# Down weights quantised after an expert's silu products, thirteen gate and up tiles quantised in attention 2, four result buffers

## The chip, the cores and the metric

The kernel runs on one core of one Trainium2 chip. The metric is the device time of the whole program in microseconds (us), as the median over runs. One execution was also taken by the hardware profiler; its span runs from the first to the last instruction.

The engines are TensorE (PE: matmuls; PEld: its weight loads), VectorE (DVE), ScalarE (ACT), GpSimd (POOL) and SyncE (SP), which here only issues DMAs.

## The reference

Eight sequences of 100 tokens with 512 features (800 rows in all) pass through four blocks, each on a layer norm of `x` and each added to `x`:

```python
x = x + L0_xattn(layernorm(x), ctx)   # 16 heads of 32, causal, 100 keys
x = x + L0_ffn(layernorm(x))          # mixture of 8 experts, top 2, hidden size 352
x = x + L1_xattn(layernorm(x), ctx)   # "attention 2": 16 heads, latent keys, 361 keys, rope
x = x + L1_ffn(layernorm(x))          # quantised ffn, hidden size 1408
```

An expert computes `silu(x W1^T) * (x W2^T)` and multiplies that by `W3^T`; each token takes its two best experts, weighted by a softmax over the two scores.

The last block works on integers. Rows of `x`, of the hidden values and of both weight matrices are divided by a scale (their largest magnitude over 127), rounded, and the product is scaled back:

```python
scale = max(max(abs(v), axis=-1) / 127.0, 1e-8)
q = clip(round(v / scale), -127, 127)
```

Its weights are `w_gate_up` (2816 x 512: 22 tiles of 128 rows) and `w_down` (512 x 1408: 4 tiles of 128 rows).

## The kernel before

The program runs through its stages in order: attention 1 with the routing of tokens (up to about 143 us of the span), the experts (to about 283 us), the projections for attention 2, attention 2 over the eight sequences ("batches"; about 345 to 536 us), and the quantised ffn over seven row tiles, the output projection of attention 2 beside it (to the end).

*Weights of the last block.* They are quantised long before they are used, beside other stages. One gate and up tile (`gu`, 128 x 512) is loaded by SP, then VectorE takes the row maximum (`amax`, L147), makes scale and inverse (L135, L138), scales and rounds (L142) and writes bf16 integers (`gu_q`, L143); SP then turns it by a transposing DMA into `w1q` (L152). A down tile (`dn`, 128 x 1408) goes the same way through `dn_q` into `w2q`. `dn` and `dn_q` have one buffer each, so the next down tile is loaded only after the one before is quantised. The constant `LATER` says how many of the 22 gate and up tiles are left for attention 2; the others go through the experts, at most two for each expert (`quantise_next`), with three tiles in flight.

*One expert.* Up to 240 token rows, gathered into slots, were turned into columns (`xgT`) during the expert before. The hidden size is cut into three groups; `gate_and_up(m)` does the products of one (L1109), ScalarE applies silu (L1120, L1128), and VectorE multiplies into `hT` (L1121; for the third group L1129 to L1133). Then TensorE turns the rows of the next expert (L1040); their copies into `xgT` are shared, the first slot block by ScalarE (L1044), the second by VectorE (L1042). VectorE makes six small values for the next expert's gates and places (`choices`, L1025 to L1031). The down matmuls (L1175) read `hT`, and the results `y` (L1185 on ScalarE, L1183 on VectorE) are added to `x_acc` by scattering DMAs from POOL (L1186). Experts 0 to 3 also carry pieces of a weight fold for attention 2 (`fold_beside`, `fold_turn`, `fold_second`, `fold_third`).

In this stage the order of TensorE, VectorE and ScalarE is the order of the code (`manual_schedule`). SP is not in that list: its DMAs are put in order by the scheduler, and each waits in the queue behind the ones before it. An expert's weights are loaded two experts ahead into two buffers (L484, L487), the slot rows too (L1015).

*Attention 2.* Each batch has 13 tiles of scores: a matmul (L1379), the maximum (L1381), the exponential on ScalarE (L1385), the reciprocal and the scaling (L1387, L1388, on VectorE or POOL in turn), transposes (L1394), the values (L1406). At tiles 3 and 9 of a batch after the first, code for one of the left gate and up tiles is placed; here the scheduler may move instructions. The context of the next batch is turned at L1285, and batches 1, 3, 5 compute the next pair's queries (L1361).

*End of the last block.* Results of a row tile are scaled into `y` (L1668), the residual is added (L1671) and the tile is written out (L1672). `y` comes from a pool with two buffers. In the tail VectorE, ScalarE and TensorE again keep the order of the code.

Of the kernel before, what the change touches and what calls it, by code (L numbers as in the profile page):

```python
# [12 lines left out]
F32 = mybir.dt.float32  # L13
# [6 lines left out]
P = 128  # L20
B, S, D = 8, 100, 512
N = B * S
L, DC = 361, 128
KC = D // P
# [26 lines left out]
def tile_kernel(  # L51
# [9 lines left out]
    def open_pool(name, bufs=1, side="left"):  # L61
        guard = tc.tile_pool(name=name, bufs=bufs, side=side)
        pool = guard.__enter__()
        return pool, lambda: guard.__exit__(None, None, None)
# [6 lines left out]
    def bank(dtype=F32):  # L71
        cols = 512 if dtype == F32 else 1024
        return psum.tile([P, cols], dtype, tag="bank", name="bank")
# [653 lines left out]
    def fold_beside(i, wq_p, kq_p, qr_p):  # L727
        pa = bank()
        for c in range(CQ // P):
            for j in range(2):  # L730
                nc.tensor.matmul(
                    pa[ds(R1 * j, R1), :P], qr_p[:, j, c, :], kq_p[:, j, c, :],
                    start=(c == 0), stop=(c == CQ // P - 1),
                )
        t_p = fw.tile([P, P], F32, tag="t_p", name=f"t_p{i}", bufs=1)
        nc.scalar.copy(t_p, pa[:, :P])
        return i, wq_p, t_p
# [115 lines left out]
    def load_down(n):  # L853
        w = qin.tile([P, NI], F32, tag="dn", name=f"dn{n}", bufs=1)
        nc.sync.dma_start(w, wdn[ts(n, P), :])
        return n, w
# [21 lines left out]
    def turn_down(n, q):  # L878
        turn_by_dma(w2q[:, :, ts(n, P)], q)

    qin, close_qin = open_pool("weights_in")
    slot_rows, close_slot_rows = open_pool("slot_rows", bufs=2)
    LATER = 9
    gate_up_left = list(range(OT - LATER))
    HC = len(SLOTS)
    GB = 3
# [2 lines left out]
    def quantise_next():  # L889
        if gate_up_in:  # L890
            turn_gate_up(*quantise_gate_up(*gate_up_in.pop(0)))
            if gate_up_left:
                gate_up_in.append(load_gate_up(gate_up_left.pop(0)))
# [118 lines left out]
    def fetch(e, tiles=None):  # L1012
        got = []
        for i, xg in enumerate(tiles or slot_tiles(e)):
            d = nc.sync.dma_start(xg, x_slot[ds(1 + e * CAP + SLOTS[i][0], SLOTS[i][1]), :])  # L1015
            got.append((xg, d.ins))
        return got
# [63 lines left out]
    down_in = load_down(0)  # L1081
# [20 lines left out]
    for e in range(NE):  # L1102
        w12_e, w3_e = experts.pop(e)
        xgT = turned
        hT = ffw.tile([P, 3, CAP], F32, tag="hT", name=f"hT{e}")

        def products(po, cols, c0=0, c1=KC):
            for c in range(c0, c1):
                nc.tensor.matmul(  # L1109
                    po, w12_e[:, c, cols], xgT[:, c, :], start=(c == c0), stop=(c == c1 - 1)  # L1110
                )

        def gate_and_up(m):
            m0, mr = HCH[m]
            pw = bank()
            s = ffw.tile([P, CAP], F32, tag="silu", name="silu")
            if m < 2:
                products(pw[:, :CAP], ds(m0, P))
                products(pw[:, ds(CAP, CAP)], ds(UP[m], P))
                nc.scalar.activation(s, pw[:, :CAP], AF.Silu)  # L1120
                nc.vector.tensor_tensor(hT[:, m, :], s, pw[:, ds(CAP, CAP)], ALU.mult)  # L1121
                return
            products(pw[:, :CAP], ds(m0, P))
            for half in range(2):
                products(
                    pw[ds(64 * half, 64), ds(CAP, CAP)], ds(UP64, 64), 2 * half, 2 * half + 2
                )
            nc.scalar.activation(s[:mr], pw[:mr, :CAP], AF.Silu)  # L1128
            nc.vector.tensor_tensor(hT[64:mr, m, :], s[64:mr], pw[mr:, :CAP], ALU.mult)  # L1129
            up = ffw.tile([64, CAP], F32, tag="up", name="up", bufs=1)  # L1130
            nc.vector.tensor_copy(up, pw[:64, ds(CAP, CAP)])
            nc.vector.tensor_tensor(up, up, pw[64:, ds(CAP, CAP)], ALU.add)
            nc.vector.tensor_tensor(hT[:64, m, :], s[:64], up, ALU.mult)  # L1133

        slots.pop(e)
        if e + 2 < NE:
            slots[e + 2] = fetch(e + 2)
        part = None
        gate_and_up(0)
        if loaded:  # L1140
            part = fold_beside(*loaded.pop(0))
            if pairs_left:
                loaded.append(fold_load(pairs_left.pop(0)))
        quantise_next()
        gate_and_up(1)
        if part:
            part = fold_turn(*part)
        if e < KC:
            turn_down(*quantise_down(*down_in))
            if e + 1 < KC:  # L1150
                down_in = load_down(e + 1)
        gate_and_up(2)
        if part:
            part = fold_second(*part)
        quantise_next()
        if e + 2 < NE:
            experts[e + 2] = load_expert(e + 2)
        else:
            load_wo(*((0, 1, 2) if e + 2 == NE else (3, 4)))
        if e == KC + 1:  # L1160
            load_wo(5, 6, 7)
        if e + 1 < NE:
            turned = columns_of(e + 1, slots[e + 1])
            gates_next = choices(e + 1, slots[e + 1])
        if part:
            fold_third(*part)

        py = [bank() for _ in range(HC)]
        down = [(m, i) for m in range(len(HCH)) for i in range(HC)]
        if e == NE - 1:  # L1170
            down.sort(key=lambda a: a[1])
        for m, i in down:
            mr = HCH[m][1]
            s0, n = SLOTS[i]
            nc.tensor.matmul(  # L1175
                py[i][:n], hT[:mr, m, ds(s0, n)], w3_e[:mr, m, :], start=(m == 0), stop=(m == 2)
            )
        for i in range(HC):
            gate, place = gates[i]
            n = SLOTS[i][1]  # L1180
            y = rows.tile([P, D], F32, tag="xn", name=f"y{e}_{i}")[:n]
            if i % 2:
                nc.vector.tensor_scalar(y, py[i][:n], gate, None, ALU.mult)  # L1183
            else:
                nc.scalar.activation(y, py[i][:n], AF.Copy, scale=gate)  # L1185
            d = nc.gpsimd.indirect_dma_start(  # L1186
                out=x_acc, out_offset=bass.IndirectOffsetOnAxis(ap=place[:, 0:1], axis=0),
                in_=y, in_offset=None, compute_op=ALU.add,
            )
            tc.declare_no_dep(  # L1190
                d.ins, group=f"expert{e}", reason="a token has one slot at most of an expert"
            )
            tc.add_to_no_dep_group(f"expert{e}", d.ins)
        gates = gates_next
# [147 lines left out]
    a1w, close_a1w = open_pool("attn1w", bufs=2)  # L1342
    late_loads = [load_gate_up(OT - LATER + i, a1w) for i in range(2)]

# [89 lines left out]
    for b in range(B):  # L1434
# [7 lines left out]
        for i, (k0, r) in enumerate(BTILES):  # L1442
            e = scores(qe, kvT, k0, r, i % 2)
# [31 lines left out]
    f2w, close_f2w = open_pool("ffn1w", bufs=2)  # L1475
# [154 lines left out]
    def down4(t, hqT, sh):  # L1630
        pd = bank()
        for i, (g, c) in enumerate(CHUNKS4):
            for j in range(4):
                nc.tensor.matmul(
                    pd[ds(R4 * j, R4), :QD], hqT[:, c, ds(R4 * g, R4)], w2q[:, i, ts(j, QD)],
                    start=(i == 0), stop=(i == IT - 1),
                )
        y = f2w.tile([P, D], F32, tag="y", name="y")
        for j in range(4):
            nc.vector.scalar_tensor_tensor(  # L1640
                y[:R4, ts(j, QD)], pd[ds(R4 * j, R4), :QD], sh[:R4],
                swb[:R4, ds(OT * P + j * QD, QD)], ALU.mult, ALU.mult,
            )
        nc.vector.tensor_tensor(y[:R4], y[:R4], xs[t][:R4], ALU.add)
        nc.sync.dma_start(out[ds(t * P, R4), :], y[:R4])
# [17 lines left out]

    def finish_rows(t, pd, sh, y=None, cols=slice(0, D)):
        if y is None:
            y = f2w.tile([P, D], F32, tag="y", name="y")
        scale = swb[:, OT * P :]
        nc.vector.scalar_tensor_tensor(  # L1668
            y[:, cols], pd[:, cols], sh, scale[:, cols], ALU.mult, ALU.mult
        )  # L1670
        nc.vector.tensor_tensor(y[:, cols], y[:, cols], xs[t][:, cols], ALU.add)  # L1671
        nc.sync.dma_start(out[ts(t, P), cols], y[:, cols])  # L1672
# [60 lines left out]
    hqT = columns_of_hidden(t, q)  # L1733
    for u, _, s, pd in waiting[1:]:
        finish_rows(u, pd, s)
    y = f2w.tile([P, D], F32, tag="y", name="y")
    for cols in (slice(0, D // 2), slice(D // 2, D)):
        pd = bank()
        down_part(pd, hqT, 0, IT, cols)
# [71 lines left out]
```

## Time and profile before

| what | value |
|---|---|
| median of 3 runs | 674.64 us (672.87 to 675.77) |
| the profiled execution: its time | 681.28 us |
| the profiled execution: its span | 679.5 us |
| mean granted TensorE clock | 0.973 |
| ScalarE and POOL busy | 245.0 and 183.5 us |
| DMA traffic | 80.35 MB, mean 118 GB/s over the span |
| transposing DMA of a down tile, time on SP's queue (4 of them) | 4.1 to 8.2 us |
| transposing DMA of a gate and up tile (22 of them) | 1.2 to 3.4 us |

How to read it: the profiled execution is one run, and sums made from its durations belong to its own time. A group row of the profile names the line, the engine, the operation, the written and the read tile, how often it ran, its busy time and its idle time with what ended it. A row of the waits names who waited, on which line, for whom, then the total in us, how often, and the longest. A row of a timeline has the start and the length in us. A line number can be that of a helper, such as L147, which serves gate and up tiles as well as down tiles; the tile's name tells them apart.

### The profile page before, as it was taken

Reading aid. Unit: us, or ns where it says so; the run is one execution under the profiler, and the core shown is the slowest. Engines: PE = TensorE matmul, PEld = TensorE weight load, DVE = VectorE, ACT = ScalarE, POOL = GpSimd, SP = SyncE. Lnnn points to the kernel's source line nnn. Section 1 sums busy time; section 2 is a strip of 40 time slices with the busy share of each in tenths; the row PEclk is TensorE's granted clock in tenths of the full one; section 3 lists DMA queues with packets and bytes.
Section 4 is the critical chain, followed back from the end, with each engine's and each line's share of the span. In section 5 each row is a group of like instructions: output and inputs, shape, how many; then the busy total and the mean of one; then the engine's idle time right before and its main releaser. Section 6 shows DMA issues by size and latency. Waiting matters only on the chain.

```text
span 679.5 us, 9904 instructions
## 1 busy us (share of the span) xinstructions
PE 646.9 (95%) x3476; PEld 415.3 (61%) x3483; DVE 419.9 (62%) x1065; ACT 245.0 (36%) x565; POOL 183.5 (27%) x196
## 2 busy tenths in 40 slices
PE   8999997889998999999989999999999999999994
PEld 5766755666655677568866666666666544444442
DVE  4875697326655553353148877876677356666687
ACT  3654544322222111232145555555555313222140
POOL 2222231501110122138514243244234102221020
PEclk9999999589999999999989999999999999999998
DMA  9700393699999998654200211110000210011211
GB/s 292 249 18 17 119 322 108 241 309 220 299 295 302 253 326 214 140 175 120 84 1 15 59 44 21 53 36 12 0 13 0 90 38 20 18 30 29 49 37 63
DMA packets 80290, 80.35 MB, mean 118 GB/s; under 512 B 41267, under 2 KB 54119, under 8 KB 80111
## 3 DMA queue, kind: packets, MB, share of 16 engines
q1 hardware_dynamic: 76543, 70.97, 36.6%
q0 software_dynamic: 3696, 8.72, 6.0%
q8 instruction: 29, 0.48, 0.3%
q14 instruction: 22, 0.18, 0.1%
HBM read 56.36 MB, written 16.50 MB: 107 GB/s over the span
## 4 chain that ended last, share of the span: by engine, by line
PE 63%; DVE 7%; DMA 7%; POOL 1%; issue 1%; ACT 1%; SPq 0%; ACTq 0%; POOLq 0%; DVEq 0%
PE bank L359 12%; PE bank L1406 9%; PE bank L1379 9%; PE bank L1109 8%; PE bank L1325 6%; PE bank L1175 5%; PE bank L1394 5%; PE bank L1539 3%; DMA dn<-in_wdn 2%; PE bank L1361 1%; DMA gu<-in_wgu 1%; DMA qr_p<-in_wqr 1%; POOL e L1388 1%; DVE amax L147 1%; PE bank L711 1%
## 5 line engine op out<-in xcount | busy, mean ns | idle before, releaser
L1388 POOL TENSOR_SCALAR e<-e,rs 128x361 f32<-128x361 f32 (+1 forms) x56 | 67.2, 1201 | 131.9 <-DVE rs L1387 118.7
L359 PE MATMUL bank<-wvo,ctxT 128*128 128x512 f32 x192 | 83.9, 593 | 0.0
L1379 PE MATMUL bank<-kvT,qe 128*128 128x361 f32 (+1 forms) x208 | 83.0, 483 | 0.1
L1109 PE MATMUL bank<-xgT,w 128*128 128x240 f32 (+1 forms) x384 | 76.5, 373 | 1.6 <-ACT xgT L1044 0.9
L1109 PEld LDWEIGHTS bank<-xgT,w 128*128 128x128 f32 (+1 forms) x384 | 64.7, 183 | 14.4 <-issue 5.6
L1406 PE MATMUL bank<-pT,kvr 121*128 121x400 f32 x192 | 70.3, 502 | 1.0 <-DVE pT L80 1.0
L1394 PEld LDWEIGHTS bank<-ident,e 128*121 128x121 f32 (+1 forms) x312 | 48.3, 186 | 34.2 <-POOL e L1388 7.3
L1385 ACT ACTIVATE e<-bank,nm 128x361 f32<-128x361 f32 (+1 forms) x104 | 58.7, 565 | 27.2 <-DVE nm L1381 18.9
L1381 DVE TENSOR_REDUCE nm<-bank 128x1 f32<-128x361 f32 (+1 forms) x104 | 54.9, 528 | 15.8 <-PE bank L1379 14.6
L359 PEld LDWEIGHTS bank<-wvo,ctxT 128*128 128x128 f32 x192 | 36.2, 190 | 43.0 <-issue 42.6
L1186 POOL DMA_INDIRECT x_acc<-y,place x16 | 24.5, 1530 | 129.9 <-ACT y L1185 126.2
L1394 PE MATMUL bank<-ident,e 128*121 128x128 f32 (+1 forms) x312 | 53.0, 280 | 3.1 <-POOL e L1388 3.0
L1556 POOL TENSOR_TENSOR hid<-g,u 128x512 f32<-128x512 f32 (+1 forms) x17 | 20.5, 1216 | 111.0 <-ACT g L1547 74.8
L1175 PE MATMUL bank<-w,hT 128*128 128x512 f32 (+3 forms) x96 | 44.3, 607 | 4.0 <-DVE hT L1133 4.0
L1406 PEld LDWEIGHTS bank<-pT,kvr 121*128 121x128 f32 x192 | 33.9, 190 | 20.2 <-ACT pT L82 0.7
L1325 PE MATMUL bank<-xT,wqf 128*128 128x256 f32 (+1 forms) x192 | 43.8, 389 | 0.7 <-ACT xT L1310 0.7
L82 ACT COPY pT<-bank 121x384 f32<-121x384 f32 (+1 forms) x63 | 28.2, 447 | 42.4 <-PE bank L1394 42.3
L324 POOL TENSOR_TENSOR s<-s,rs 100x800 f32<-100x800 f32 x16 | 24.4, 1522 | 70.0 <-DVE rs L323 30.5
L1325 PEld LDWEIGHTS bank<-xT,wqf 128*128 128x128 f32 x192 | 36.3, 190 | 7.4 <-ACT xT L1310 0.9
L80 DVE COPY ctxT<-bank 128x400 f32<-128x400 f32 (+2 forms) x31 | 17.7, 572 | 37.0 <-PE bank L1325 26.0
L1379 PEld LDWEIGHTS bank<-kvT,qe 128*128 128x128 f32 (+1 forms) x208 | 32.9, 189 | 10.7 <-DVE rs L1387 0.5
L1175 PEld LDWEIGHTS bank<-w,hT 128*128 128x128 f32 (+3 forms) x96 | 16.8, 184 | 25.1 <-issue 16.6
(259 smaller groups left out, 1004.2 us busy)
## 6 DMA issues: line engine op xcount, KB each, us to landing
w<-in_w SPq DMA_DIRECT2D x8, 1408.0 KB
gu<-in_wgu SPq DMA_DIRECT2D x22, 256.0 KB
w<-in_w SPq DMA_DIRECT2D x16, 256.0 KB
wq_p<-in_wq SPq DMA_DIRECT2D x8, 512.0 KB
wo<-in_wo SPq DMA_DIRECT2D x8, 512.0 KB
x_slot<-zeros SPq DMA_DIRECT2D x1, 3840.0 KB
kq_p<-in_wkcq SPq DMA_DIRECT2D x16, 192.0 KB
dn<-in_wdn SPq DMA_DIRECT2D x4, 704.0 KB
```

Source lines behind the costliest of these rows:

```text
L82: nc.scalar.copy(dst, src)
L359: nc.tensor.matmul(po[:, :D], lhs[:, c, ds(t * P, r)], rhs[:, c, :], start=(c == 0), stop=(c == chunks - 1),)
L1109: nc.tensor.matmul(po, w12_e[:, c, cols], xgT[:, c, :], start=(c == c0), stop=(c == c1 - 1))
L1175: nc.tensor.matmul(py[i][:n], hT[:mr, m, ds(s0, n)], w3_e[:mr, m, :], start=(m == 0), stop=(m == 2))
L1186: d = nc.gpsimd.indirect_dma_start(out=x_acc, out_offset=bass.IndirectOffsetOnAxis(ap=place[:, 0:1], axis=0), in_=y, in_offset=None, compu ...
L1325: nc.tensor.matmul(pq[:, i, :], wqf[:, c, ts(p0 + i, P)], xT[:, c, :], start=(c == 0), stop=(c == KC - 1),)
L1379: nc.tensor.matmul(ps[:r, :L], qe[:, ds(k0, r)], kvT, start=True, stop=True)
L1381: d = nc.vector.tensor_reduce(nm[:r], ps[:r, :L], AX.X, ALU.max, negate=True)
L1385: nc.scalar.activation(e[:r], ps[:r, :L], AF.Exp, bias=nm[:r], accum_out=sm[:r])
L1388: (nc.vector if odd else nc.gpsimd).tensor_scalar_mul(e[:r], e[:r], rs[:r])
L1394: nc.tensor.transpose(pt[:LP, c, :r], e[:r, ds(c * (LP - 1), LP)], ident[:r, :r])
L1406: nc.tensor.matmul(pc[:, :VC], kvr[:, c, :], pT[:, c, :], start=(c == 0), stop=(c == LC - 1))
```

## The change

Three edits. In the experts, the quantisation of a down tile moves from between `gate_and_up(1)` and `gate_and_up(2)` to behind `gate_and_up(2)`, and from experts 0 to 3 to experts 1 to 4; the first down tile is still loaded before the experts begin, and the load of the next one follows the quantisation as before. `LATER` becomes 13, so nine gate and up tiles go through experts 0 to 4 (two in each of the first four, one in expert 4) and thirteen through attention 2. The result tile `y` of the last block gets four buffers. The order of instructions on TensorE, ScalarE and POOL is that of before; VectorE's and SP's change.

```diff
-    LATER = 9
+    LATER = 13
     gate_up_left = list(range(OT - LATER))
...
         gate_and_up(1)
         if part:
             part = fold_turn(*part)
-        if e < KC:
+        gate_and_up(2)
+        if 0 < e <= KC:
             turn_down(*quantise_down(*down_in))
-            if e + 1 < KC:
-                down_in = load_down(e + 1)
-        gate_and_up(2)
+            if e < KC:
+                down_in = load_down(e)
         if part:
             part = fold_second(*part)
         quantise_next()
...
-        y = f2w.tile([P, D], F32, tag="y", name="y")
+        y = f2w.tile([P, D], F32, tag="y", name="y", bufs=4)
...
-            y = f2w.tile([P, D], F32, tag="y", name="y")
+            y = f2w.tile([P, D], F32, tag="y", name="y", bufs=4)
...
-    y = f2w.tile([P, D], F32, tag="y", name="y")
+    y = f2w.tile([P, D], F32, tag="y", name="y", bufs=4)
```

## The prediction

> **What bounds the kernel now.** I read the page's busy row first, then the waits of TensorE and VectorE, then the chain of work that ended last, then the stretches that the change touches instruction by instruction. TensorE sets the pace: 646.9 of 679.5 us busy. What can be won is its 32.6 us of idleness and the time at a lower clock (mean granted clock 0.973, so about 0.027 x 679.5 = 18 us).
>
> ```profile
> PE 646.9 (95%) x3476; PEld 415.3 (61%) x3483; DVE 419.9 (62%) x1065; ACT 245.0 (36%) x565; POOL 183.5 (27%) x196
> ```
>
> Now the waits: TensorE's in the stretch 150 to 290 us (the experts), then VectorE's over the span (total, times, longest).
>
> ```profile
> PE bank L1175 <- DVE hT L1133: 4.0, 3, 2.9
> PE bank L1109 <- issue: 0.7, 1, 0.7
> ...
> DVE amax L147 <- DMA dn<-in_wdn: 7.4, 2, 4.7
> ...
> DVE y L1668 <- DMA out_y<-y: 0.7, 1, 0.7
> ```
>
> VectorE twice stood before the maximum of a down weight tile (`dn`) whose load had not landed; behind it in VectorE's queue stood the silu products `hT`, for which TensorE's down matmuls waited. The chain shows both places and what followed (start, length):
>
> ```profile
> 182.76 8.93 DMA dn<-in_wdn
> 191.72 1.63 DVE amax L147
> ...
> 207.03 6.35 DMA dn<-in_wdn
> 213.39 1.63 DVE amax L147
> ...
> 219.10 2.85 PE bank L1175 x4
> 221.94 9.97 PE bank L1109 x48
> ...
> 238.06 9.07 PE bank L1109 x48
> ```
>
> The same 48 matmuls took 9.97 us after the second stall and 9.07 later. So I price the loss by periods between starts of gate and up products (timeline of TensorE): 162.89 to 180.50 = 17.61 us for an undisturbed expert with a fold (1, 2 and 3 have one), 237.89 to 253.10 = 15.21 without. Experts 1 to 4 took 162.89 to 237.89 = 75.0 us against 3 x 17.61 + 15.21 = 68.04. **The loss before is L = 7.0 us**, gaps and slow clock together.
>
> **Part 1, down weights behind the silu products.** Nothing is added: four times five VectorE instructions (1.61 + 0.15 + 0.16 + 0.95 + 0.89), a transposing DMA and (three times) a load move from experts 0 to 3 into experts 1 to 4, and within an expert from before the last gate and up group to after its products. `hT` never waits for `dn` any more: the 4.0 us row should go. What is late next: the integers now stand between `hT` and the next expert's `xgT` copy, and its first products need `xgT`. VectorE's timeline of expert 1 before:
>
> ```profile
> 171.35 1.61 DVE L147 TENSOR_REDUCE amax<-dn 128x1 f32<-128x1408 f32 x1
> ...
> 175.29 0.41 DVE L1129 TENSOR_TENSOR hT<-silu,bank 32x240 f32<-32x240 f32 x1
> ...
> 176.92 0.67 DVE L147 TENSOR_REDUCE amax<-gu 128x1 f32<-128x512 f32 x1
> ...
> 178.99 0.62 DVE L1042 COPY xgT<-bank 128x448 f32<-128x448 f32 x1
> ```
>
> From it: `dn` block 171.35 to 175.29 = 3.94 us, gate and up tile 176.92 to 178.99 = 2.07, copy 0.62. The silu of the third group starts at 173.29 (ACT); in expert 4, where VectorE is free, VectorE is through with the products 2.03 us after that silu starts (231.97 to 234.00). So the new chain is 173.29 + 2.03 + 3.94 + 2.07 + 0.62 = 181.95, and TensorE starts 0.11 us after such a copy (199.98 to 200.09): 182.06 against 180.50. **Each of experts 1, 2 and 3 gains a stall of 1.56 us**, however early `dn` lands, because before this block started 4 us earlier, beside the third group's matmuls. In expert 4 there is no second gate and up tile any more: 231.97 + 2.03 + 3.94 + 0.62 + 0.11 = 238.67 against 237.89, 0.78. Together 5.5 us in place of L.
>
> Other engines behind the moved block: six small choice instructions and `y` (0.75 us) follow the copy and come 2 to 3 us later than before; their scatter on POOL has over an expert to land. On SP the transposing DMA held the queue 4.1 to 8.2 us before, and the third-matrix loads, row fetches and the next `dn` load stand behind it. In expert 1 it can issue at 179.3; `dn` 1 is then asked for at 183.4 to 187.5 and, at the 6.35 to 8.93 us seen, lands at 189.8 to 196.4. It is due at 182.06 + 10.40 (start of products to third silu, 162.89 to 173.29) + 2.03 = 194.5. Only the worst of both ends is late, by 2 us; I take 0, since a megabyte of gate and up tiles leaves this stretch. The other things behind it are due an expert later or more.
>
> Does a 1.5 us gap cost clock as well? Windows of the trace (length, busy times, then PEclk, DMA share, GB/s):
>
> ```profile
> 199.00:201.00 2.00, 1.32 (x6) 0.89 (x6) 1.90 (x9) 0.27 (x1) 1.45 (x1) 1.00 1.17 217
> ...
> 221.00:222.00 1.00, 1.00 (x3) 0.27 (x2) 0.93 (x6) 0.00 (x0) 0.76 (x1) 0.50 1.05 406
> ...
> 353.00:355.00 2.00, 2.00 (x8) 1.46 (x8) 1.06 (x4) 0.00 (x0) 0.86 (x1) 0.55 0.00 0
> ```
>
> After gaps of 0.87 and 0.68 us within 3.6 us the clock stayed at 1.00; after one gap of 2.88 and one of 2.27 us it fell to about half. [...] by the rows, a gap of 1.56 us lies between the cases. Its price is 0 or, by 9.97 against 9.07 us, 0.9 us for each of three. I take 0, because 1.55 us of idleness in 3.6 us did nothing, and keep +2.7 for the range.
>
> **Part 2, thirteen tiles for attention 2.** Four loads of 256 KB, four short transposing DMAs and 4 x 2.07 us of VectorE leave experts 4, 5 and 6. Beyond expert 4 this gains nothing: expert 5, with two such tiles, has the same 15.21 us period as expert 6 with one. They arrive in batches that had one or none. TensorE's transposes of the context mark the batches (start, length):
>
> ```profile
> 365.76 0.47 PE L1285 MATMUL bank<-ident,kvr 121*128 121x121 f32 x3
> 390.56 0.47 PE L1285 MATMUL bank<-ident,kvr 121*128 121x121 f32 x3
> 412.27 0.47 PE L1285 MATMUL bank<-ident,kvr 121*128 121x121 f32 x3
> 437.26 0.47 PE L1285 MATMUL bank<-ident,kvr 121*128 121x121 f32 x3
> 459.25 0.47 PE L1285 MATMUL bank<-ident,kvr 121*128 121x121 f32 x3
> 484.00 0.47 PE L1285 MATMUL bank<-ident,kvr 121*128 121x121 f32 x3
> 505.72 0.47 PE L1285 MATMUL bank<-ident,kvr 121*128 121x121 f32 x3
> ```
>
> Batches with queries: 24.80 and 24.99 with two tiles, 24.75 with none. Without: 21.71 with two, 21.99 with one, 21.72 with none. A tile costs nothing to 0.3 us, since TensorE's work covers VectorE (39 of 50 us busy there). If that cover were gone it would be the whole 8.3 us. I take +0.5 for four, 0 to 1.2 for the range. On SP their transposes stand before loads of the context that have 10 us to spare. The last tile is turned tens of us before its first use at 550.6.
>
> **Part 3, four result buffers.** In the tail VectorE is the chain. The wait of 0.66 us before the `y` at 672.71 (the last row of the waits above) is for the output DMA of the tile two earlier; with four buffers it is gone and all after it comes earlier: -0.7. What follows on VectorE is back to back, so nothing else is exposed.
>
> **The sum** against the profiled execution: -7.0 + 5.5 + 0.5 - 0.7 = -1.7, a span of 677.8. That execution took 681.28 us, 6.6 more than the median 674.64 of the runs. [...] runs without the profiler must have less of the 32.6 + 18 = 51 us of idleness and slow clock, 13% less in proportion. Scaling L alike gives 6.1, while the 5.5 is VectorE's own work and stays. My forecast for the median is 674.64 - 6.1 + 5.5 + 0.5 - 0.7, **673.8 us**, which is no change that counts: 0.5% (3.4 us) is about what a measurement of this kernel can tell.
>
> **Rivals.**
> - *The late loads are mostly the profiled execution's (0.22).* L depends on loads in a stretch with its DMA engines full (share 1.0 to 1.2). If they land in time otherwise, L is near 0 and the stalls at `xgT` are bought for nothing: +5.5 + 0.5 - 0.7 = +5.3, or 679.9. The change loses when L is under 5.3 and by over 0.5% when it is under 1.9. For it: 2.7 and 4.7 us less lateness are enough to empty both stalls, and without the gap of 2.88 us the slow clock goes too. Against: `dn` 3 hung on an 8.2 us transpose and a 6.35 us load, more than profiling would explain. Likely within it: 676.5 to 680.
> - *The clock falls at the new gaps (0.10):* +2.7 on the forecast, 676.5.
> - *The new order makes `dn` late again (0.05),* behind the product loads on SP: 2 us for each of three, 680.
> - *More is won (0.08):* L in full and lighter traffic, and by chance of timing the 2.27 us gap at the start of attention 2 without its slow clock (4 us at 0.57, 1.7 us): 674.64 - 1.7 - 1.7 = 671.2.
>
> **How the numbers follow.** The likeliest case has 0.55 and reaches from 672.3 to 675.7. Faster by over 0.5% takes the last rival and a little of the likeliest: 0.12. Slower takes most of the first and third and a little of the second: 0.22. The rest is 0.66. The range is 670.8 to 679.2: the low end just takes in the last rival, the high end nearly all of the first.
>
> **What would show it.** Right: no wait of L1175 for `hT`; in its place L1109 waits at the starts of experts 2, 3 and 4 for about 1.5 us and of expert 5 for 0.8, with VectorE's `xgT` copy as releaser, clock 1.00 there; periods of 19.2 us for experts 1 to 3 and 16.0 for expert 4; batch periods as above within 0.3 us; no wait of `y` for `out_y`. Wrong: `amax` still waiting for `dn`, a clock of 0.5 after these gaps, `e` of POOL or `pT` waited for in batches 4 to 6, or products of experts waiting for their weights.

## The result: slower by 0.6%, with the stall that was forecast

The changed kernel takes 678.99 us (median of 7 runs, 677.11 to 681.69); the kernel before takes 675.51 in 7 runs of its own. The ratio of the times is 1.0064 with an interval of 1.004 to 1.0087, so about +4.3 us (+2.7 to +5.9); it compares fast runs only and leaves out one slow run of before (683.45 us), so it is not the quotient of the two medians. The forecast was 673.8 us, 0.8 below the median of before then known, and no change that counts.

The two profiles said the opposite. The changed kernel's profiled execution took 678.07 us with a span of 676.3, the one of before 681.28 with 679.5. A reader who compares only these two sees a gain of 3 us.

The waits of the changed kernel, first TensorE's (total, times, longest). They answer to the rows of L1175 and L1109 shown of before:

```profile
PE bank L1109 <- issue: 4.6, 4, 1.4
...
PE bank L1175 <- DVE hT L1133: 0.3, 1, 0.3
```

The wait for the silu products is gone but for the 0.3 us of the last expert. In its place the products L1109 stand still four times. No row of VectorE's waits names `dn` or `out_y` any more. The four places in TensorE's timeline (start, length, and in brackets the idle time before):

```profile
181.38 3.48 PE L1109 MATMUL bank<-xgT,w 128*128 128x240 f32 x16 [1.28 <-issue]
...
200.58 3.48 PE L1109 MATMUL bank<-xgT,w 128*128 128x240 f32 x16 [1.35 <-issue]
...
219.78 9.31 PE L1109 MATMUL bank<-xgT,w 128*128 128x240 f32 x48 [1.36 <-issue]
...
235.83 9.31 PE L1109 MATMUL bank<-xgT,w 128*128 128x240 f32 x48 [0.60 <-issue]
```

These are the starts of experts 2, 3, 4 and 5. The profile calls the wait "issue", that is, it found no releaser. VectorE's timeline in expert 1 shows what TensorE waits for:

```profile
174.75 1.60 DVE L147 TENSOR_REDUCE amax<-dn 128x1 f32<-128x1408 f32 x1
...
178.57 0.68 DVE L147 TENSOR_REDUCE amax<-gu 128x1 f32<-128x512 f32 x1
...
180.65 0.62 DVE L1042 COPY xgT<-bank 128x448 f32<-128x448 f32 x1
```

The down block runs from 174.75 to 178.57, the gate and up tile follows, and the copy of the next expert's columns ends at 181.27; the products start at 181.38, the 0.11 us later that the prediction read from before. So the "issue" of the profile is a wait for VectorE here; e6 and e7 below test that. From the start of expert 1 to that of expert 5 it is 162.33 to 235.83 = 73.5 us; the prediction's 68.04 + 5.5 is the same number. The four gaps add up to 4.6 us of the 5.5. The other 0.9 comes with them: a group that starts without a gap starts 0.16 us before the row ahead of it ends (before: down matmuls from 175.34 for 5.32 us, products at 180.50), and behind a gap the first sixteen products take 3.48 us instead of 3.40.

The batches of attention 2, by the second and the eighth row of the transposes L1285, six batch periods apart:

```profile
362.51 0.47 PE L1285 MATMUL bank<-ident,kvr 121*128 121x121 f32 x3
...
503.44 0.47 PE L1285 MATMUL bank<-ident,kvr 121*128 121x121 f32 x3
```

That is 140.93 us, against 505.72 - 365.76 = 139.96 before. From the last of these rows to the end of the span it is 172.86 us, against 173.78.

So where do the profiled 3.2 us come from? Experts 1 to 4: 73.5 instead of 75.0, because the 7 us of late loads were in that one execution of before. Start of attention 2 (first to second transposes L1285): 20.02 us instead of 21.28, with a granted clock of 1.00 instead of 0.55 in the 2 us window behind its idle gap, taken up in the last section. The end: 0.92. Up to the start of expert 1: 0.56. Batches: -0.97 (the changed kernel's are longer). In sum 3.3, less 0.1 between expert 5 and the first L1285 row.

### The profile page after: what moved, and what is told of

It is laid out like the page before. It is cut to its first block, busy times and chain, and to the rows that moved or that the text cites. A ratio compares the mean times of both kernels' runs of the same rounds, so it can differ in the third digit from the quotient of the medians.

```text
span 676.3 us, 9919 instructions
## 1 busy us (share of the span) xinstructions
PE 643.7 (95%) x3483; PEld 412.9 (61%) x3483; DVE 416.0 (62%) x1065; ACT 244.5 (36%) x565; POOL 184.3 (27%) x196
## 4 chain that ended last, share of the span: by engine, by line
PE 67%; DVE 6%; DMA 3%; issue 2%; POOL 2%; ACT 1%; SPq 0%; ACTq 0%; POOLq 0%; DVEq 0%
PE bank L359 12%; PE bank L1109 11%; PE bank L1406 9%; PE bank L1379 8%; PE bank L1325 6%; PE bank L1175 6%; PE bank L1394 5%; PE bank L1539 3%; PE bank L1214 2%; DMA gu<-in_wgu 2%; POOL e L1388 1%; DMA qr_p<-in_wqr 1%; PE bank L1040 1%; PE bank L1361 1%; PE bank L711 1%
## 5 line engine op out<-in xcount | busy, mean ns | idle before, releaser
L1109 PE MATMUL bank<-xgT,w 128*128 128x240 f32 (+1 forms) x384 | 75.7, 370 | 5.5 <-issue 4.6
L1109 PEld LDWEIGHTS bank<-xgT,w 128*128 128x128 f32 (+1 forms) x384 | 63.8, 181 | 18.2 <-issue 11.0
L1175 PE MATMUL bank<-w,hT 128*128 128x512 f32 (+3 forms) x96 | 43.0, 595 | 0.3 <-DVE hT L1133 0.3
L1121 DVE TENSOR_TENSOR hT<-silu,bank 128x240 f32<-128x240 f32 x16 | 6.5, 404 | 41.0 <-ACT silu L1120 41.0
```

The costliest lines, as they stand in the source:

```text
L1109: nc.tensor.matmul(po, w12_e[:, c, cols], xgT[:, c, :], start=(c == c0), stop=(c == c1 - 1))
L1175: nc.tensor.matmul(py[i][:n], hT[:mr, m, ds(s0, n)], w3_e[:mr, m, :], start=(m == 0), stop=(m == 2))
```

## The experiments

Two theories stood after the result. Theory 1: an ordinary execution of before loses almost nothing to late down weights, so the 5.5 us of new stalls are paid for nothing. Theory 2: the 7 us are lost every time, and the change costs some 6 us elsewhere. Four kernels were run together, each timed against the kernel before. Only the ratios and the stretches within a profile are compared with the first two profiles, not the times in us: in these runs the kernel before itself has a median of 678.39 us beside e1 to e4 and of 677.79 beside e5 to e8, and expert 1 starts at 165.4 to 168.5 us instead of 162.3 to 162.9. In the edits, `(quantise)` stands for the lines that quantise, turn and load a down tile.

### e1: the kernel before, once more

No edit.

> The kernel before once more, unchanged, to get a second profile of it. Theory 1 (the late loads of the down weights in the first profile were exceptional, an ordinary execution loses little by them): VectorE's waits for dn sum to under 3 us instead of 7.4, experts 1 to 4 take 68 to 70 us instead of 75.0, and the profiled execution lies within 3 us of the median. Theory 2 (the 7 us are lost in every execution, and the change costs some 6 us elsewhere, in attention 2 or the last block): 7 us of waits and 75 us again. Time ratio 1.000 either way.

Measured: ratio 1.0013 (0.9988 to 1.0038). Its profile: VectorE's wait for `dn`, then TensorE's for `hT`.

```profile
DVE amax L147 <- DMA dn<-in_wdn: 0.8, 1, 0.8
```

```profile
PE bank L1175 <- DVE hT L1133: 0.3, 1, 0.3
```

And the starts of experts 1 and 5 in TensorE's timeline:

```profile
166.44 3.40 PE L1109 MATMUL bank<-xgT,w 128*128 128x240 f32 x16
...
234.67 9.23 PE L1109 MATMUL bank<-xgT,w 128*128 128x240 f32 x48
```

68.23 us, so L was 0.2 us in this execution (68.23 - 68.04) and not 7.0. The span was 674.9 us instead of 679.5. Theory 1 stands. The difference lies on SP. Counted from the start of expert 1, the load of `dn` 2 was issued at 15.8 us here (182.28) and at 19.9 in the first profile (182.76), that of `dn` 3 at 34.6 (201.00) and at 44.1 (207.03). The transposing DMA in front of `dn` 3 held SP for 4.27 us here and for 8.21 there. The first difference on SP's queue is earlier, at the transposing DMA of the first down tile (first and third tile, in the first profile, then here):

```profile
157.63 4.68 SPq L152 DMA_TRANSPOSE w2q<-dn_q  x1
...
198.77 8.21 SPq L152 DMA_TRANSPOSE w2q<-dn_q  x1
```

```profile
161.19 1.70 SPq L152 DMA_TRANSPOSE w2q<-dn_q  x1
...
196.67 4.27 SPq L152 DMA_TRANSPOSE w2q<-dn_q  x1
```

The one of the first tile was issued 5.26 us before the start of expert 1 there and 5.25 here, but held SP 3 us longer there (in e3, e4 and e8 it held it for 1.83 to 1.96 us). The load of `dn` 1 behind it then came 3.0 us later, that of `dn` 2 4.0 and that of `dn` 3 9.6. Why that one transfer held the queue for 4.68 us is not settled by these runs.

### e2: only the down weights moved

```diff
-        if e < KC: (quantise)
         gate_and_up(2)
+        if 0 < e <= KC: (quantise)
```

> Only the down weights' integers move behind the silu products and to experts 1 to 4; nine tiles stay left for attention 2 and two result buffers. Expert 4 then has its second gate and up tile too. Theory 1: four stalls of about 1.3 to 1.5 us before the next expert's products and nothing won in return, so +4 to +6 us, ratio 1.006 to 1.009. Theory 2: the stalls replace the 7 us, so -1 us, ratio 0.998.

Measured: ratio 1.0131 (1.0093 to 1.0169), 685.68 us in 6 runs, so about +8.9 us (+6.3 to +11.5). Theory 2 falls. The cost is above what theory 1 had said, and the trace shows where. The waits before experts 2 to 4 are 1.28, 1.28 and 1.36 us as expected, but in expert 4 the second gate and up tile is still there, and no fold work of TensorE covers it:

```profile
242.37 9.31 PE L1109 MATMUL bank<-xgT,w 128*128 128x240 f32 x48 [2.68 <-issue]
```

Experts 1 to 4 take 75.50 us, 7.3 more than in e1; that is inside the interval. So the larger `LATER` does earn something once the block has moved: it takes 2.07 us out of the chain of expert 4.

### e3: only thirteen tiles for attention 2

```diff
-    LATER = 9
+    LATER = 13
```

> Only thirteen instead of nine gate and up tiles left for attention 2; the down weights and the result buffers as before. Theory 1: between -1 and +1 us, ratio 0.9985 to 1.0015. Theory 2: attention 2 pays, +4 us or more, ratio 1.006 or above.

Measured: ratio 0.9993 (0.9974 to 1.0013). Theory 2 falls here too: attention 2 does not pay. Experts 1 to 4 take 68.03 us.

### e4: only four result buffers

```diff
-        y = f2w.tile([P, D], F32, tag="y", name="y")
+        y = f2w.tile([P, D], F32, tag="y", name="y", bufs=4)
```

> Only the four result buffers. Both theories: the wait of y for out_y goes and nothing else moves, -0.7 us, ratio 0.999.

Measured: ratio 0.9989 (0.9963 to 1.0015), which does not settle a gain of 0.7 us. The trace does: no wait of `y` for `out_y`, and 172.91 us from the last L1285 row to the end (677.3 - 504.39), against 173.73 in e1 (674.9 - 501.17).

The second four kernels ask why the stall is there and what would avoid it. e5, e6 and e7 start from the changed kernel, e8 from the kernel before.

### e5: the block back in its old place, experts 1 to 4 kept

```diff
         gate_and_up(1)
         ...
+        if 0 < e <= KC: (quantise)
         gate_and_up(2)
-        if 0 < e <= KC: (quantise)
```

> The changed kernel, its down weights' integers put back in front of the third gate and up group but kept in experts 1 to 4. Theory A (the cost is the place in VectorE's queue, between the silu products and the next expert's columns): no wait of the products for the columns, experts 1 to 4 take 68 to 69 us instead of 73.5, ratio to before 0.997 to 1.000. Rival B (the cost is the shift by one expert, or the order of DMAs that comes with it): the 1.3 us waits or late loads stay, ratio 1.005 to 1.008.

Measured: ratio 1.0021 (0.9997 to 1.0046), between the two expectations. The waits of the products for the columns are gone, up to expert 4: its start at 218.86 is 52.83 us after that of expert 1 (166.03), exactly three undisturbed periods. So it is the place in VectorE's queue that makes the stall, not the shift by one expert. But in expert 4 a down tile came late, and rival B has its part. VectorE, then TensorE:

```profile
231.82 1.62 DVE L147 TENSOR_REDUCE amax<-dn 128x1 f32<-128x1408 f32 x1 [5.42 <-DMA dn<-in_wdn]
```

```profile
237.52 3.78 PE L1175 MATMUL bank<-w,hT 96*128 96x512 f32 x4 [5.01 <-DVE hT L1133]
```

The load was issued at 218.72 and landed 13 us later. Expert 4 has no fold and is 2.4 us shorter, so the load that hangs on expert 3's block has less time; that this is why it was late is not shown. The loss has the form of that in the first profile, in another expert.

### e6: the block behind the next expert's columns

```diff
-        if 0 < e <= KC: (quantise, behind gate_and_up(2))
...
             gates_next = choices(e + 1, slots[e + 1])
+        if 0 < e <= KC: (quantise)
```

> The changed kernel, the down weights' integers moved further back, behind the copy of the next expert's columns and the six small choice instructions. Theory A: VectorE then has until the next expert's first silu, the 1.3 us waits go and nothing waits for the block, 68 to 69 us for experts 1 to 4, ratio to before 0.997 to 1.000. Rival C (the block costs its 3.9 us wherever it stands behind the third group, since VectorE has no room there): y and its scatter come late and the next products wait, ratio 1.004 or more.

Measured: ratio 0.9976 (0.9959 to 0.9992), 676.56 us. Theory A holds, rival C falls: experts 1 to 4 take 68.03 us (166.35 to 234.38). Here too a down tile was late, by 2.24 us:

```profile
234.81 1.62 DVE L147 TENSOR_REDUCE amax<-dn 128x1 f32<-128x1408 f32 x1 [2.24 <-DMA dn<-in_wdn]
```

and TensorE did not notice, because behind the block there stand only `y` and work of the next expert; the next products start on time:

```profile
219.17 9.23 PE L1109 MATMUL bank<-xgT,w 128*128 128x240 f32 x48
...
234.38 9.23 PE L1109 MATMUL bank<-xgT,w 128*128 128x240 f32 x48
...
249.59 9.23 PE L1109 MATMUL bank<-xgT,w 128*128 128x240 f32 x48
```

Both periods are the undisturbed 15.21 us.

### e7: only the second gate and up tile behind the columns

```diff
-        quantise_next()   (in front of the columns of the next expert)
...
             gates_next = choices(e + 1, slots[e + 1])
+        quantise_next()
```

> The changed kernel, with only the expert's second gate and up tile (2.07 us of VectorE) moved behind the copy of the next expert's columns; the down weights stay as changed. Theory A, by the chain's arithmetic: the stall of 1.3 us in experts 1 to 3 falls by 2.07 us, so to nothing, and the 0.6 us of expert 4 stays, since it has no such tile; experts 1 to 4 take 68.6 us, ratio to before 0.998 to 1.001. Rival C: the stalls stay at 1.3 us.

Measured: ratio 1.0017 (0.999 to 1.0045). The arithmetic of the chain holds: 2.07 us out of it, and the stalls of experts 1 to 3 are gone (start of expert 4 at 219.34, 52.83 us after 166.51). The last one is larger than the expected 0.6 us:

```profile
236.53 9.31 PE L1109 MATMUL bank<-xgT,w 128*128 128x240 f32 x48 [1.82 <-issue]
```

1.06 us of that is a wait of VectorE for the last down tile, which was late in this execution. Rival C falls.

### e8: the other two edits without the move

```diff
-    LATER = 9
+    LATER = 13
...
+    y = f2w.tile([P, D], F32, tag="y", name="y", bufs=4)   (three places)
```

> The kernel before with two of the three edits: thirteen tiles for attention 2 and four result buffers, the down weights as before. Theory A: the sum of the two singles, ratio to before 0.997 to 0.999, the best of all so far. Rival D (the edits only pay or cost together): 1.003 or more.

Measured: ratio 0.9972 (0.9952 to 0.9992), 677.0 us. Rival D falls. Both e6 and e8 are faster than the kernel before by 0.2 to 0.3%, with intervals that end below 1 and lie almost on each other, and so, by their ratios to it, than the changed one.

### The pieces side by side

From the profiles: experts 1 to 4 (start of expert 1 to start of expert 5), six batch periods (second to eighth L1285 row), and the end behind them.

| kernel | down block | experts 1 to 4 | six batch periods | end | ratio to before |
|---|---|---|---|---|---|
| before, first profile | old place | 75.0 | 139.96 | 173.78 | |
| e1, before again | old place | 68.23 | 139.89 | 173.73 | 1.0013 |
| e3, LATER | old place | 68.03 | 140.14 | 173.76 | 0.9993 |
| e4, y | old place | 68.04 | 139.86 | 172.91 | 0.9989 |
| e8, LATER and y | old place | 68.03 | 139.46 | 172.89 | 0.9972 |
| changed | behind `hT` | 73.50 | 140.93 | 172.86 | 1.0064 |
| e2, move | behind `hT` | 75.50 | 139.99 | 173.75 | 1.0131 |
| e5 | old place, one expert later | 75.06 | 140.05 | 172.89 | 1.0021 |
| e6 | behind the columns | 68.03 | 139.93 | 172.92 | 0.9976 |
| e7 | behind `hT`, tile moved | 70.02 | 140.77 | 172.85 | 1.0017 |

Of five profiles with the block in its old place and experts, four lose 0.0 to 0.2 us by late down weights and one loses 7.0. The result itself says the same of the executions timed there: with 7.0 us lost in each of them the pieces would add up to -2.1 us, and +4.3 (+2.7 to +5.9) was measured. The single times agree with an event that comes in some executions only. Of e5's 22 executions six took 683 us or more, the others at most 680.5; the profiled one, with its late load, is among the six (683.47). Of the 67 of before beside e5 to e8, seven took 683 us or more, of the 22 of e6 none. But e8, with the block in its old place too, has one in 22, and only the profiled executions show what made them long: that the long ones of before are those with late loads is not shown.

## Why the prediction was wrong

The direction was wrong, though the median of 678.99 us lies inside the stated range of 670.8 to 679.2, whose high end was set to take in the first rival. The step that failed is the scaling of L. The prediction priced what the change takes away, L, from one execution at 7.0 us, and carried it to ordinary executions in proportion to all idleness and slow clock: 13% less, 6.1; that the 6.6 us lay in those two, spread evenly, was the author's estimate. In e1, e3, e4 and e8 it is 0.0 to 0.2 us. So the loss is not spread over the executions in proportion: with the block in its old place it is next to nothing in four profiles and 7.0 us in the one that was priced. The prediction named this as its first rival (L near 0, +5.3 us, 679.9) and gave it 0.22; what came is that rival, at +4.3. The proportion rested on the thought that it is the profiler that makes an execution longer. e1's profiled execution took 676.69 us, less than the median 678.51 of its own kernel, so profiling need not make it longer; the 6.6 us by which the first one was longer are about the 7.0 that it lost to late loads. The argument against the rival, that an 8.2 us transposing DMA and a 6.35 us load are more than profiling explains, was no argument either: nothing in one profile says how often such a pair occurs.

The other steps, as the table and the rows show:

- *Stalls at the columns.* 5.5 us forecast; 73.5 - 68.04 = 5.5 measured, with periods of 19.05, 19.20, 19.20 and 16.05 us where 19.2 and 16.0 were forecast. The mechanism and the sum were right, and so was "however early `dn` lands". e6 and e7 show the cause by taking the block or the tile out of the chain.
- *No more wait of the down matmuls for `hT`.* Right: 0.3 us is left, and it is in e1 as well.
- *Down weights not late again in the new order.* Right for the changed kernel. Its transposing DMAs of down tiles held SP for 1.4 to 1.7 us and not the assumed 4.1 to 8.2, and the load of `dn` 1 was asked for at 180.46, 3 us before the early end of what the prediction allowed (183.4). It is not so in every execution: in e7, with the block in the same place, the last down tile came 1.06 us late.
- *Clock at the new gaps.* Right: none of the gaps up to 1.36 us lowered it. The granted clock is 1.00 (third number from the end) in the 2 us behind each of the four, as behind the second:

```profile
201.00:203.00 2.00, 2.00 (x12) 1.88 (x11) 0.90 (x3) 0.00 (x0) 0.83 (x1) 1.00 1.18 369
```

- *Four more tiles in attention 2.* +0.5 forecast. The six kernels with thirteen tiles take 140.2 us for the six periods in the mean, the four profiles with nine 139.9: +0.3, less than the six differ among themselves (139.46 to 140.93). The two long ones, the changed kernel and e7, have a wait of TensorE for `pT` in their first period (0.61 and 0.94 us) that e8, with the same tiles, does not have.
- *Result buffers.* -0.7 forecast, -0.8 to -0.9 in the six kernels that have them.

With L = 0.2, as in e1, and the measured pieces the same sum gives -0.2 + 5.5 + 0.3 - 0.9 = +4.7 us, inside the measured +2.7 to +5.9.

## What to carry to other kernels

A stall that hangs on a late transfer, seen in one profile, may be an event of that execution (here 7.0 us in one profile of the kernel before and 0.2 in the next): before an edit is paid for with certain work on a critical chain, profile the unchanged kernel a second time. Work that only fills an engine's idle time belongs behind everything that the pacing engine will wait for next: the same five instructions cost 5.5 us in front of the next expert's columns and nothing behind them. And a move is to be checked against the next consumer in the queue, not only against the one that it frees.

## What the runs showed of the hardware

In these runs the granted clock did not follow from the length of a gap alone. At the start of attention 2 every one of the ten profiles has the same idle gap, of 2.27 or 2.28 us. After it the clock fell in five of them (before, e2, e4, e6, e7) and stayed at 1.00 in the other five, such as the changed kernel: over the stretch 345 to 370 us its mean is 0.93 in each of the first five and 1.00 in each of the others. The gap before and in the changed kernel, and the window behind the second (the prediction shows that of before, 353 to 355 us, with 0.55):

```profile
352.76 0.62 PE L1394 MATMUL bank<-ident,e 128*121 128x128 f32 x3 [2.27 <-POOL e L1388]
```

```profile
350.77 0.59 PE L1394 MATMUL bank<-ident,e 128*121 128x128 f32 x3 [2.27 <-POOL e L1388]
```

```profile
351.00:353.00 2.00, 1.91 (x10) 1.09 (x9) 1.54 (x6) 0.67 (x2) 0.88 (x1) 1.00 0.00 0
```

The stretch from the first to the second L1285 row is 20.0 us where it stayed and 21.0 to 21.4 where it fell. In e2 the granted clock was 1.00 behind the gap of 2.68 us, in e5 it was 0.50 behind the one of 5.01 us; the windows behind them:

```profile
243.00:245.00 2.00, 2.00 (x12) 1.88 (x11) 0.69 (x2) 0.00 (x0) 1.03 (x1) 1.00 0.75 134
```

```profile
238.00:240.00 2.00, 2.00 (x3) 0.64 (x3) 0.81 (x7) 0.37 (x1) 0.00 (x0) 0.50 1.03 397
```

So gaps of 2.27 us went both ways. The gap of 2.88 us in the first profile of before, of which the prediction has the window at 0.50, was followed by a lower clock, and the one of 2.68 us in e2 was not. What decides it, no run shows. What the lower clock costs at the start of attention 2, about 1.0 to 1.4 us for a gap of 2.27 us (21.0 to 21.4 against 20.0), is a quarter to a third of the measured 4.3 us, and it moves between executions of one and the same kernel: 21.28 us for that stretch in the first profile of before, 20.02 in e1.
